# Transposing q, k and x with VectorE blocks and SBUF-to-SBUF DMAs instead of TensorE, in a fused attention and feed-forward kernel

## The chip, the cores and the metric

The kernel runs on one core of one Trainium2 chip. The metric is the device time of one execution in microseconds (us); lower is better. Before the change the median of three runs is 1325.62 us (1324.89 to 1325.84).

The names of the engines in the profile: PE is TensorE's matmul, PEld its weight load, DVE is VectorE, ACT is ScalarE, POOL is GpSimd, SP is SyncE, which here only issues DMAs. A q behind a name (SPq) is the engine's sequencer.

## The reference

128 short sequences of 32 positions with 512 channels go through one layer: a conditional mixing of channels, attention with a causal linear bias, an adapter matrix chosen by sequence, and a feed-forward part with a shared and a routed branch. All is float32.

```python
# _L0_cond_ref: each sequence has its own 32x32 matrix
W = weights[condition]
x1 = jnp.einsum('bct,bcd->bdt', x, W)

# _L0_attn_ref: 32 heads of 16
qkv = jnp.clip(jnp.einsum('bsd,ed->bse', x1, w_qkv), -8.0, 8.0)
q, k, v = jnp.split(qkv, 3, axis=-1)
q = _layer_norm(q, q_ln_w, q_ln_b)
k = _layer_norm(k, k_ln_w, k_ln_b)
scores = jnp.einsum('bqhd,bkhd->bhqk', q, k) * scale      # per head
scores = jnp.where(causal, scores + slopes * rel, -jnp.inf)
attn = jnp.einsum('bhqk,bkhd->bqhd', softmax(scores), v)
x = x + jnp.einsum('bsd,ed->bse', attn, w_out)

# _L0_cond2_ref: each sequence has its own 512x512 adapter
h = jnp.einsum('bsi,boi->bso', x, weight[adapter_ids])

# _L0_ffn_ref
top2 = jax.lax.top_k(jnp.einsum('bsh,he->bse', h, gate_w), 2)[0]
shared = jnp.einsum('bsi,ih->bsh', relu(h @ up_w) ** 2, down_w)
routed = ((h @ fc1_w) @ expert_w * sum(top2)) @ fc2_w
x = x + _layernorm(shared + routed, ln_gamma, ln_beta)
```

## The kernel before

The 4096 rows are cut into 32 tiles of 128 rows (128 partitions), so a tile holds four sequences of 32 positions (SEQ = 4, S = 32). Its 512 channels are four chunks of 128 (DC = 4). One loop runs over t = 0 to 33. In step t, tile t goes through its attention and its adapter, tile t+1 is mixed and projected ahead of it, and the feed-forward of tiles t-2 and t-3 is dealt out in eight pieces called fill(0) to fill(7): in even steps the eight column blocks of `up` for a pair of tiles (moving 256 columns at once), in odd steps the eight quarters of `down`, four for each tile of the pair.

What a tile passes through, with the lines that the profile names:

- `load` (L160, L162): x by a DMA on SP's queue, the condition's matrix by an indirect DMA on POOL's. `load_adapters` (L173, L190): the four sequences' ids into SP's registers, then eight DMAs of 512 KB on SP's queue into buffers that adapt of the tile before has to leave first.
- `mix` (L205, L213, L218): a block-diagonal mask by POOL, four matmuls (pxc), one copy to xcT by ACT.
- `project` (L230, L236, L242, L243): for i = 0, 1, 2 (q, k, v) four matmuls of 128x512, a clip by VectorE out of PSUM, and for q and k the statistics of the layer norm. `normalise` (L249): the layer norm without its weights, after a root by ACT and a reciprocal by VectorE (`rstd_of`, L153, L155).
- `turn` (L261, L263): eight 128x128 transposes of k and q by TensorE into two PSUM banks (pk, pq). `scale` (L273, L278, L282): the layer norm's weights, now per partition, by VectorE for k and by ACT for q, and kx, k copied out four times under a head mask.
- `scores` (L299, L306), `exponent` (L316, L317, L322), `share` (L327, L329, L330), `flip` (L338): q times k by heads, bias, maximum (VectorE), subtraction (POOL), exponential (ACT), sum and reciprocal (VectorE), product (POOL), and a transpose in 32x32 blocks by VectorE.
- `spread` (L349): v under a sequence mask by POOL. `weigh` (L362, L373): the probabilities times v (po), turned in blocks by VectorE (aT). `attend` (L382, L386): the output projection (pw), added to x by VectorE.
- `turn_x` (L392, L394, L395): four transposes of x by TensorE (px), a copy to xT by ACT, and POOL adds beta to x. `adapt` (L411, L416): for each of the four sequences in turn sixteen small matmuls with that sequence's adapter, and a VectorE transpose in 32x32 blocks into hT, which gathers the blocks in another order.
- `route` (L430, L437 to L443): the gate and the routed branch in two halves. `up` (L450, L455, L456) and `down` (L464). `finish` (L475 to L488): the sum, its layer norm and the store; `down` calls it after its last quarter. `routed_inner` and `routed_outer` multiply the routed branch's weights together once, at the start.

The instructions are written in an order by hand (the calls ahead of the loop and in it). The framework puts each on its engine's queue and sets the semaphores; where an operand comes late it may put a later, ready instruction first. Each queue then runs strictly in order. DMAs of SP's queue use eight semaphores in turn, so one waits until the DMA eight before it has landed. Dependencies go by the part of a tile that is read or written. PSUM has eight banks, which are handed out in turn.

Of the kernel before, what the change touches and what calls it, by code (L numbers as in the profile page):

```python
# [17 lines left out]
P = 128  # L18
# [12 lines left out]
NE = 8  # L31
# [10 lines left out]
def adaln_attn_ffn(  # L42
# [27 lines left out]
    def bank(name):  # L70
        return ps.tile([P, 512], F32, tag="ps", name=name)


    ident = const.tile([P, P], F32, name="ident")
    make_identity(nc, ident)
    eps = const.tile([P, 1], F32, name="eps")
# [168 lines left out]
    def normalise(t):  # L245
        s = tiles[t]
        r = rstd_of(s["mv"], 2, f"qk_{t}")
        for i in range(2):
# [4 lines left out]
            )  # L253

    def turn(t):

        s = tiles[t]
        s["pk"] = bank(f"pk_{t}")
        s["pq"] = bank(f"pq_{t}")
        for c in range(DC):  # L260
            nc.tensor.transpose(s["pk"][:, ts(c, P)], s["qk"][:, 1, ts(c, P)], ident)  # L261
        for c in range(DC):
            nc.tensor.transpose(s["pq"][:, ts(c, P)], s["qk"][:, 0, ts(c, P)], ident)  # L263

    def scale(t):

        s = tiles[t]
        s["qT"] = w1.tile([P, DC, P], F32, tag="qT", name=f"qT_{t}")
        kT = w1.tile([P, DC, P], F32, tag="kT", name=f"kT_{t}")

        s["kx"] = w1.tile([P, DC, SEQ, HQ, S], F32, tag="kx", name=f"kx_{t}")
        for c in range(DC):
            nc.vector.tensor_scalar(  # L273
                out=kT[:, c, :], in0=s["pk"][:, ts(c, P)],
                scalar1=lnc[:, 2, c : c + 1], scalar2=lnc[:, 3, c : c + 1],
                op0=ALU.mult, op1=ALU.add,
            )
            nc.scalar.activation(  # L278
                s["qT"][:, c, :], s["pq"][:, ts(c, P)], AF.Identity,
                bias=qaff[:, 1, c : c + 1], scale=qaff[:, 0, c : c + 1],  # L280
            )
            nc.vector.tensor_tensor(  # L282
                out=s["kx"][:, c],
                in0=kT[:, c, :].rearrange("p (b k) -> p b k", b=SEQ).unsqueeze(2)
                .broadcast_to([P, SEQ, HQ, S]),
                in1=m_half.unsqueeze(1).unsqueeze(3).broadcast_to([P, SEQ, HQ, S]),
                op=ALU.mult,
            )

    def scores(t):  # L290
# [4 lines left out]
        for c in range(DC):  # L295
            for b in range(SEQ):
                for r in range(2):
                    rows_r = slice(r * P // 2, (r + 1) * P // 2)
                    nc.tensor.matmul(  # L299
                        banks[r][ts(b, S), ts(c, HQ * S)],  # L300
                        lhsT=s["qT"][rows_r, c, ts(b, S)],
                        rhs=s["kx"][rows_r, c, b].rearrange("p h k -> p (h k)"),
                        start=True, stop=True,
                    )
# [53 lines left out]
    def weigh(t):  # L358
# [12 lines left out]

        s["aT"] = w1.tile([P, DC, SEQ, S], F32, tag="kT", name=f"aT_{t}")
        nc.vector.transpose(  # L373
# [14 lines left out]
    def turn_x(t):  # L388
        s = tiles[t]
        px = bank(f"px_{t}")  # L390
        for c in range(DC):
            nc.tensor.transpose(px[:, ts(c, P)], s["x"][:, ts(c, P)], ident)  # L392
        s["xT"] = w1.tile([P, DC, P], F32, tag="qT", name=f"xT_{t}")
        nc.scalar.copy(s["xT"].rearrange("p c n -> p (c n)"), px)  # L394
        nc.gpsimd.tensor_tensor(out=s["x"], in0=s["x"], in1=bet_sb, op=ALU.add)  # L395

    def adapt(t):
# [10 lines left out]
        for j in range(SEQ):  # L408
            for c in range(DC):
                for g in range(DC):  # L410
                    nc.tensor.matmul(  # L411
                        pad[ts(g, S), ts(j, P)], lhsT=s["xT"][:, c, ts(j, S)],
                        rhs=s["adw"][c // 2][j][:, c % 2, ts(g, P)],
                        start=(c == 0), stop=(c == DC - 1),
                    )
# [43 lines left out]
    def down(t, quarter):  # L459
# [3 lines left out]
        for f in range(2 * quarter, 2 * quarter + 2):  # L463
# [3 lines left out]
            )  # L467
        if quarter == 3:
            finish(t)

    def finish(t):

        s = tiles.pop(t)
        y = s["y"]
        nc.vector.tensor_tensor(out=y, in0=y, in1=s["pd"], op=ALU.add)  # L475
        st = sm.tile([P, 6], F32, tag="st", name=f"stf_{t}")
        nc.vector.bn_stats(out=st, in_=y)
        mv = sm.tile([P, 1, 2], F32, tag="mv1", name=f"mvf_{t}")
        nc.vector.bn_aggr(out=mv[:, 0, :], in_=st)
        r = rstd_of(mv, 1, f"f_{t}")  # L480
# [11 lines left out]
    load(0)  # L492
    for c in range(DC):
        for i in range(3):
            nc.sync.dma_start(
                out=wqkv_sb[:, c, ts(i, D)], in_=w_qkvT[c * P : (c + 1) * P, ts(i, D)]
            )
    load(1)
# [3 lines left out]
    for c in range(DC):  # L502
        for i in range(3):
            project(0, i, (c,))
    normalise(0)
    spread(0)
    nc.sync.dma_start(out=lnc, in_=ln_cols)
# [9 lines left out]
    load_adapters(0)  # L517
    nc.sync.dma_start(out=bet_sb, in_=beta.broadcast_to([P, D]))

    for g in range(DC):  # L520
        nc.sync.dma_start(
            out=rout_sb[ts(g, S), :, :NE], in_=gate_w[:, g, :].rearrange("(e d) n -> d e n", d=S)
        )
    for g in range(DC):
        nc.sync.dma_start(
            out=up_sb[ts(g, S), :, :],
            in_=up_w[g * P : (g + 1) * P, :].rearrange("(e d) f -> d e f", d=S),
        )
    nc.sync.dma_start(out=down_sb, in_=down_w.rearrange("(c p) f -> p c f", p=P))
    nc.sync.dma_start(out=gam_sb, in_=gamma.broadcast_to([P, D]))  # L530

# [4 lines left out]
    for t in range(NTILE + GRP):  # L536
        here, ahead, ffn = t < NTILE, t + 1 < NTILE, t >= GRP
        g = t // GRP - 1

        def fill(i):  # L540
            if t == 0 and i >= 4:
                routed_outer(i - 4)
            elif t == 1 and i == 3:
                mix(3)
            elif t == 1 and i >= 4:
                project(3, 0, (i - 4,))
            elif ffn and t % GRP == 0:
                up(g, i)
            elif ffn:
                down(g * GRP + i // 4, i % 4)  # L550

        if t + 2 < NTILE:
            load(t + 2)
        when(here and t > 0, load_adapters, t)
        when(here, turn, t)
        when(here, scale, t)
        when(ahead and t != 2, mix, t + 1)
        fill(0)
        fill(1)
        when(ffn, route, t - GRP, 0)  # L560
        when(here, scores, t)
        when(here, exponent, t)
        when(ffn, route, t - GRP, 1)
        when(ahead and t != 2, project, t + 1, 0)
        when(here, share, t)
        when(ahead, project, t + 1, 1)
        when(here, flip, t)
        fill(2)
        when(ahead, project, t + 1, 2)
        fill(3)  # L570
        when(here, weigh, t)
        when(ahead, normalise, t + 1)
        when(ahead, spread, t + 1)
        fill(4)
        when(here, attend, t)
        fill(5)
        when(here, turn_x, t)
        fill(6)
        fill(7)
        when(here, adapt, t)  # L580


# [75 lines left out]
```

## Time and profile before

| | us |
|---|---|
| median of the runs (3) | 1325.62 |
| the profiled execution | 1324.37 |
| its span, first to last instruction | 1322.4 |
| TensorE matmul busy (share 97%) | 1285.9 |
| VectorE busy (48%) | 640.6 |
| GpSimd busy (34%) | 447.0 |
| ScalarE busy (23%) | 303.0 |
| granted TensorE clock, mean | 0.991 |
| one step in the middle, e.g. from one px to the one two steps later, halved | 39.53 |

The costliest matmuls in the profile's groups are the projections (340.7 us busy), `up` (237.8) and `down` (237.7). Matmuls overlap in the array, so the mean duration of one (593 ns for a projection's) is longer than the distance from one to the next; distances between starts tell what a group costs. The loads from memory come to 153.93 MB, most of it adapters, 4 MB for each tile. The span can be read in three stages: up to about 101 us, where the first two tiles go through without feed-forward work; the steps 2 to 30; and from about 1243 us on, step 31 and the two last steps, which hold feed-forward work alone.

### The profile page before, as it was taken

To read this page: it belongs to the slowest core of one execution; us is meant where nothing else is said; L and a number is where in the kernel's file an instruction comes from. 1 tells how busy PE (TensorE), PEld (TensorE's weight loads), DVE (VectorE), ACT (ScalarE), POOL (GpSimd) and SP (SyncE) were. 2 spreads that over 40 slices of the span, in tenths; PEclk is the share of its full clock that TensorE was granted. 3 is DMA by queue.
4 is the path that set the end of the run, shared out by engine and by line. 5 is a ranking of instruction groups with operands and counts; after the bars stand their busy time and mean duration, and the time that the engine had idled before them with its cause. 6 is when DMAs were issued, how large, how long until landed. Compare 5 with 4: busy or idle time off the path is not lost.

```text
span 1322.4 us, 28001 instructions
## 1 busy us (share of the span) xinstructions
PE 1285.9 (97%) x11976; PEld 819.9 (62%) x11976; DVE 640.6 (48%) x1123; ACT 303.0 (23%) x552; POOL 447.0 (34%) x393
## 2 busy tenths in 40 slices
PE   5989999999999999999999999999999999999977
PEld 2447566665666756566665666756566665666655
DVE  2464553635545363653635545363653535455332
ACT  1222222121222222222121222212222121222211
POOL 4334333343323334323342324333333332323211
PEclk9989999999999999999999999999999999999989
DMA  9733343412434322343422334322343421334300
GB/s 317 201 121 127 128 161 129 141 68 97 145 129 161 129 71 90 130 159 129 159 73 76 143 129 160 129 97 75 133 146 128 161 88 74 127 128 144 128 17 16
DMA packets 51473, 164.12 MB, mean 124 GB/s; under 512 B 7061, under 2 KB 7830, under 8 KB 51350
## 3 DMA queue, kind: packets, MB, share of 16 engines
q1 hardware_dynamic: 47238, 153.15, 32.6%
q0 software_dynamic: 3424, 8.39, 1.6%
q8 instruction: 94, 1.54, 0.5%
q10 hardware_dynamic: 688, 0.79, 0.2%
q14 instruction: 29, 0.24, 0.0%
HBM read 153.93 MB, written 8.39 MB: 123 GB/s over the span
## 4 chain that ended last, share of the span: by engine, by line
PE 94%; DMA 4%; DVE 1%; issue 0%; POOL 0%; SPq 0%; ACTq 0%; POOLq 0%; DVEq 0%
PE pqkv L230 23%; PE pu L450 17%; PE pd L464 17%; PE pr L430 9%; PE pad L411 9%; PE pw L382 9%; PE psc L299 3%; PE po L362 2%; PE pxc L213 2%; PE pk L261 1%; DMA down_sb<-in_down_w 1%; PE px L392 1%; PE pq L263 1%; DMA bet_sb<-in_beta 1%; DMA fc_t<-in_fc_w 0%
## 5 line engine op out<-in xcount | busy, mean ns | idle before, releaser
L230 PE MATMUL pqkv<-wqkv_sb,xcT 128*128 128x512 f32 x768 | 340.7, 593 | 0.7 <-ACT xcT L218 0.7
L230 PEld LDWEIGHTS pqkv<-wqkv_sb,xcT 128*128 128x128 f32 x768 | 145.4, 190 | 163.7 <-issue 159.7
L450 PE MATMUL pu<-hT,up_sb 128*128 128x256 f32 x1024 | 237.8, 381 | 0.8 <-DVE hT L416 0.8
L464 PE MATMUL pd<-down_sb,act 128*128 128x512 f32 x512 | 237.7, 599 | 0.0
L450 PEld LDWEIGHTS pu<-hT,up_sb 128*128 128x128 f32 x1024 | 190.9, 190 | 45.8 <-issue 21.5
L349 POOL TENSOR_TENSOR vx<-v,msk 128x1024 f32<-128x1024 f32 x64 | 126.8, 2002 | 96.4 <-PE po L362 85.8
L464 PEld LDWEIGHTS pd<-down_sb,act 128*128 128x128 f32 x512 | 94.2, 191 | 101.6 <-issue 96.9
L456 POOL TENSOR_TENSOR act<-act 128x256 f32<-128x256 f32 x128 | 81.5, 636 | 188.9 <-ACT act L455 188.6
L430 PE MATMUL pr<-rout_sb,hT 128*128 128x256 f32 (+1 forms) x512 | 125.5, 389 | 0.0
L317 POOL TENSOR_TENSOR s<-s,mx 128x1024 f32<-128x1024 f32 x32 | 61.2, 1913 | 188.9 <-DVE mx L316 188.9
L382 PE MATMUL pw<-wout_sb,aT 128*128 128x512 f32 x256 | 117.6, 603 | 5.3 <-DVE aT L373 5.3
L411 PEld LDWEIGHTS pad<-adw,xT 128*32 128x32 f32 x4096 | 109.9, 110 | 17.7 <-issue 17.7
L455 ACT ACTIVATE act<-pu 128x256 f32<-128x256 f32 x128 | 49.2, 384 | 302.9 <-PE pu L450 302.9
L411 PE MATMUL pad<-adw,xT 128*32 128x128 f32 x4096 | 118.4, 273 | 0.0
L430 PEld LDWEIGHTS pr<-rout_sb,hT 128*128 128x128 f32 x512 | 94.8, 190 | 25.8 <-issue 13.6
L330 POOL TENSOR_TENSOR s<-s,rden 128x1024 f32<-128x1024 f32 x32 | 61.5, 1921 | 119.5 <-DVE rden L329 115.7
L236 DVE TENSOR_SCALAR qk<-pqkv 128x512 f32<-128x512 f32 x64 | 44.2, 691 | 106.1 <-PE pqkv L230 106.0
L416 DVE STREAM_TRANSPOSE hT<-pad 128x512 f32<-128x512 f32 x32 | 23.0, 717 | 145.4 <-PE pad L411 145.4
L382 PEld LDWEIGHTS pw<-wout_sb,aT 128*128 128x128 f32 x256 | 49.5, 194 | 62.6 <-issue 51.4
L282 DVE TENSOR_TENSOR kx<-kT,m_half 128x512 f32<-128x512 f32 x128 | 82.5, 684 | 0.0
L278 ACT ACTIVATE qT<-pq,qaff 128x128 f32<-128x128 f32 x128 | 48.2, 456 | 117.4 <-PE pq L263 117.4
L475 DVE TENSOR_TENSOR y<-y,pd 128x512 f32<-128x512 f32 x32 | 22.0, 688 | 99.0 <-PE pd L464 99.0
(63 smaller groups left out, 1145.1 us busy)
## 6 DMA issues: line engine op xcount, KB each, us to landing
adw<-in_adapt_w SPq DMA_DIRECT2D x256, 512.0 KB, 8.3
x<-in_x SPq DMA_DIRECT2D x32, 256.0 KB, 10.3
out<-y POOLq DMA_DIRECT2D x30, 256.0 KB, 3.6
wqkv_sb<-in_w_qkvT SPq DMA_DIRECT2D x12, 256.0 KB, 6.1
up_sb<-in_up_w SPq DMA_DIRECT2D x4, 512.0 KB, 7.7
down_sb<-in_down_w SPq DMA_DIRECT2D x1, 2048.0 KB
wout_sb<-in_w_outT SPq DMA_DIRECT2D x4, 256.0 KB, 7.9
fc_t<-in_fc_w ACTq DMA_DIRECT2D x1, 512.0 KB
```

The lines of the kernel that those rows point to most:

```text
L230: nc.tensor.matmul(s["pp", i], lhsT=s["xcT"][:, c, :], rhs=wqkv_sb[:, c, ts(i, D)], start=(c == 0), stop=(c == DC - 1),)
L282: nc.vector.tensor_tensor(out=s["kx"][:, c], in0=kT[:, c, :].rearrange("p (b k) -> p b k", b=SEQ).unsqueeze(2) .broadcast_to([P, SEQ, HQ, S]),
L317: nc.gpsimd.tensor_tensor(out=s["s"], in0=s["s"], in1=mx.unsqueeze(2).broadcast_to([P, H, S]), op=ALU.subtract,)
L330: nc.gpsimd.tensor_tensor(out=s["s"], in0=s["s"], in1=rden.unsqueeze(2).broadcast_to([P, H, S]), op=ALU.mult)
L349: nc.gpsimd.tensor_tensor(out=vx, in0=s["v"][:, ts(half, D // 2)].rearrange("p (h d) -> p h d", d=HD).unsqueeze(2) .broadcast_to([P, H // ...
L382: nc.tensor.matmul(pw, lhsT=s["aT"][:, g].rearrange("p b q -> p (b q)"), rhs=wout_sb[:, g, :], start=(g == 0), stop=(g == 3),)
L411: nc.tensor.matmul(pad[ts(g, S), ts(j, P)], lhsT=s["xT"][:, c, ts(j, S)], rhs=s["adw"][c // 2][j][:, c % 2, ts(g, P)], start=(c == 0), sto ...
L430: nc.tensor.matmul(pr[:, :n], lhsT=hT[:, c, ts(t % GRP, P)], rhs=rout_sb[:, c, ROUT[half] : ROUT[half + 1]], start=(c == 0), stop=(c == DC ...
L450: nc.tensor.matmul(pu[:, : GRP * P], lhsT=up_sb[:, c, ts(f, P)], rhs=pair["hT"][:, c, :], start=(c == 0), stop=(c == DC - 1),)
L455: nc.scalar.activation(a, pu[:, : GRP * P], AF.Relu)
L456: nc.gpsimd.tensor_tensor(out=a, in0=a, in1=a, op=ALU.mult)
L464: nc.tensor.matmul(s["pd"], lhsT=pairs[t // GRP]["acts"][f][:, ts(t % GRP, P)], rhs=down_sb[:, f, :], start=(f == 0), stop=(f == FC - 1),)
```

## The change

The transposes of `turn` and `turn_x` leave TensorE. A new helper `swap` does them in two moves: VectorE transposes every 32x32 block in place of its own (`blocks`), and 16 DMAs on SP's queue carry the blocks from one group of 32 partitions to another, j being the source group (the sequence) and i the target group. q and k go together, so one such DMA moves 32 partitions with two runs of 512 bytes; for x it is one run. The results stay in the order [sequence, chunk, position], and `scale`, `scores` and `adapt` read them so. `scale` works in place in SBUF. The identity matrix and the three PSUM banks go; aT gets a buffer of its own.

The order of the steps changes:

- `turn` and `scale` of tile t+1 are now in step t: `turn` after `normalise`, which follows `flip`, and `scale` after fill(4). A step begins with `scores`.
- `project(t+1, 2)` (v) and `spread` move behind `attend` and `turn_x`; `route`'s second half moves between `weigh` and `attend`; `project(t+1, 0)` and `(t+1, 1)` stay ahead of fill(2).
- `turn_x` comes ahead of v's projection and fill(4), where it came after fill(5).
- `finish` is cut in two: `total` (sum and statistics) at the old place, `finish` later, in the next step for the odd tile of a pair.
- Ahead of the loop the weights of q and k come before those of v, `turn(0)`, `mix(1)`, `project(1, 0)`, `project(1, 1)`, `scale(0)` and half of `routed_outer` are done; the loads of beta, gate, up, down and gamma are issued in step 0 after `turn(1)`. The work that fills steps 0 and 1 is dealt out anew.

```diff
+    def swap(srcs, name):
+        n = len(srcs)
+        blocks = w1.tile([P, n, DC, DC, S], F32, tag=f"blocks{n}", name=f"blocks_{name}")
+        out = w1.tile([P, n, SEQ, DC, S], F32, tag=f"T{n}", name=f"T_{name}")
+        for k, src in enumerate(srcs):
+            nc.vector.transpose(
+                out=blocks[:, k], in_=src.rearrange("p (c i d) -> p i c d", c=DC, i=DC)
+            )
+        for j in range(SEQ):
+            for i in range(DC):
+                nc.sync.dma_start(out=out[ts(i, S), :, j], in_=blocks[ts(j, S), :, i])
+        return out
+
     def turn(t):
         s = tiles[t]
-        s["pk"] = bank(f"pk_{t}")
-        s["pq"] = bank(f"pq_{t}")
-        for c in range(DC):
-            nc.tensor.transpose(s["pk"][:, ts(c, P)], s["qk"][:, 1, ts(c, P)], ident)
-        for c in range(DC):
-            nc.tensor.transpose(s["pq"][:, ts(c, P)], s["qk"][:, 0, ts(c, P)], ident)
+        s["T"] = swap([s["qk"][:, i, :] for i in range(2)], f"qk_{t}")
...
     def turn_x(t):
         s = tiles[t]
-        px = bank(f"px_{t}")
-        for c in range(DC):
-            nc.tensor.transpose(px[:, ts(c, P)], s["x"][:, ts(c, P)], ident)
-        s["xT"] = w1.tile([P, DC, P], F32, tag="qT", name=f"xT_{t}")
-        nc.scalar.copy(s["xT"].rearrange("p c n -> p (c n)"), px)
+        s["xT"] = swap([s["x"]], f"x_{t}")[:, 0]
         nc.gpsimd.tensor_tensor(out=s["x"], in0=s["x"], in1=bet_sb, op=ALU.add)
...
     normalise(0)
+    turn(0)
+    project(0, 2)
     spread(0)
...
     load_adapters(0)
+    mix(1)
+    project(1, 0)
+    project(1, 1)
+    scale(0)
+    for c in range(DC // 2):
+        routed_outer(c)
...
+        first = {
+            (0, 2): [(routed_outer, 2)], (0, 3): [(routed_outer, 3)],
+            (1, 2): [(project, 2, 2)], (1, 3): [(spread, 2)],
+            (1, 4): [(mix, 3)], (1, 5): [(project, 3, 0)],
+        }
+        done = {(1, 0), (1, 1), (2, 3), (3, 0)}
...
         if t + 2 < NTILE:
             load(t + 2)
         when(here and t > 0, load_adapters, t)
-        when(here, turn, t)
-        when(here, scale, t)
-        when(ahead and t != 2, mix, t + 1)
+        when(here, scores, t)
+        when(ahead and t not in (0, 2), mix, t + 1)
         fill(0)
+        when(here, exponent, t)
         fill(1)
+        when(t > GRP and t % GRP == 0, finish, t - GRP - 1)
         when(ffn, route, t - GRP, 0)
-        when(here, scores, t)
-        when(here, exponent, t)
-        when(ffn, route, t - GRP, 1)
-        when(ahead and t != 2, project, t + 1, 0)
+        look(0)
         when(here, share, t)
-        when(ahead, project, t + 1, 1)
+        look(1)
         when(here, flip, t)
+        when(ahead, normalise, t + 1)
+        when(ahead, turn, t + 1)
+        if t == 0:
+            late_loads()
         fill(2)
-        when(ahead, project, t + 1, 2)
         fill(3)
         when(here, weigh, t)
-        when(ahead, normalise, t + 1)
-        when(ahead, spread, t + 1)
+        when(ffn, route, t - GRP, 1)
+        when(here, attend, t)
+        when(here, turn_x, t)
+        when(ffn and t % GRP, finish, t - GRP - 1)
+        if t != 1:
+            look(2)
+            when(ahead, spread, t + 1)
         fill(4)
-        when(here, attend, t)
+        when(ahead, scale, t + 1)
         fill(5)
-        when(here, turn_x, t)
         fill(6)
         fill(7)
         when(here, adapt, t)
+    finish(NTILE - 1)
```

`look(i)` is `project(t + 1, i)`, left out where it is done already; `late_loads` holds the five weights' loads.

## The prediction

> **What bounds the kernel now.** I read the page from the top: busy time by slice, then the chain that ended last, then busy time by stage, then the groups of instructions, then a timeline of two steps.
>
> ```profile
> PE   5989999999999999999999999999999999999977
> DMA  9733343412434322343422334322343421334300
> PE 94%; DMA 4%; DVE 1%; issue 0%; POOL 0%; SPq 0%; ACTq 0%; POOLq 0%; DVEq 0%
> ```
>
> TensorE is busy everywhere but in the first and the last slices, and 94% of the chain lies on it. The busy time by stage makes that exact (columns: stretch, length, then busy time and instructions of PE, PEld, DVE, ACT and POOL, the granted clock, the DMA share, GB/s):
>
> ```profile
> 0.00:101.00 101.00, 78.71 (x737) 41.33 (x738) 43.67 (x69) 20.64 (x31) 37.03 (x39) 0.93 0.68 215
> 101.00:1243.00 1142.00, 1142.00 (x10792) 736.46 (x10793) 572.30 (x1007) 269.51 (x495) 398.60 (x341) 1.00 0.33 121
> 1243.00:1323.00 80.00, 65.16 (x451) 42.11 (x448) 24.62 (x48) 12.82 (x26) 11.40 (x13) 0.93 0.15 56
> ```
>
> From 101 to 1243 us TensorE isn't idle at all, at full clock. There, what is taken off TensorE comes off the time, one for one, unless a wait takes its place. VectorE is half free, the DMA engines two thirds.
>
> **What is removed.** The twelve 128x128 transposes of a tile. Their busy time, 21.4 + 19.7 + 19.3 us by their groups, counts overlaps of pipelined matmuls, so I take distances between starts instead:
>
> ```profile
> 681.76 0.60 PE L392 MATMUL px<-ident,x 128*128 128x128 f32 x4
> 682.20 3.62 PE L450 MATMUL pu<-hT,up_sb 128*128 128x256 f32 x16
> 685.75 3.70 PE L411 MATMUL pad<-adw,xT 128*32 128x128 f32 x128
> 689.38 0.65 PE L261 MATMUL pk<-ident,qk 128*128 128x128 f32 x4
> 690.31 1.06 PE L213 MATMUL pxc<-blk,x 128*128 128x128 f32 x8
> ```
>
> px costs 682.20 - 681.76 = 0.44 us, pk with pq 690.31 - 689.38 = 0.93 us: 1.37 us a tile, **43.8 us** over 32 tiles. (By the chain's shares, 1.3% + 1.1% + about 1%, it would be 45.) ACT's copy of xT (0.59) goes too, off the path.
>
> **What is added, VectorE.** Three transposes of 128x512 a tile; the nearest row is hT's, which also gathers blocks: 0.72 us, so 2.2 us in a step of 39.5 in which VectorE is busy for 20. Free in throughput; its latency is in the sums below. The scaling of k and q reads SBUF instead of PSUM; neither is on the path, as scores follow 5 us later (below).
>
> **What is added, DMAs.** 32 a tile on SP's queue, 32 KB each for q with k, 16 KB for x: 24 MB more in all, 0.75 MB a step. The DMA engines have room, and at the right place:
>
> ```profile
> 652.00:661.00 9.00, 9.00 (x99) 7.13 (x98) 5.19 (x10) 3.13 (x8) 3.36 (x5) 1.00 0.99 374
> 661.00:686.00 25.00, 25.00 (x156) 15.94 (x157) 8.82 (x15) 6.16 (x11) 11.58 (x10) 1.00 0.01 4
> ```
>
> A step's adapter matrices fill the engines for some 12 us, then nothing moves for 25. The moves of q and k fall into that gap, as they follow the second projection. What counts is how fast SP issues, since the queue keeps order: the 16 of x stand behind the 16 of q and k, and behind x the next adapters. Two lines' DMAs in the view by source line, and SP's timeline:
>
> ```profile
> L514 SPq DMA_DIRECT2D wout_sb<-in_w_outT x4: 311/312/332, 14.3 to 16.4; - x4
> L495 SPq DMA_DIRECT2D wqkv_sb<-in_w_qkvT x12: 328/434/738, 2.0 to 9.9; - x12
> 686.45 4.50 SPq L190 DMA_DIRECT2D adw<-in_adapt_w  x8
> ```
>
> (ns least, median, most.) A DMA into 32 partitions takes 0.31 us to issue (wout), one into 128 takes 0.43 (wqkv), 0.04 between two. So one costs between **0.36** and **0.47** us, or 0.56 if the 4.50 us of eight adapter loads with their register work were the measure. I take 0.36, wout's, the only ones that also fill 32 partitions. Landing: between 1.7 us (msk, 6 KB, idle engines) and 2.9 (x, 256 KB, the fastest); I take 2.0. A DMA also waits for the one eight before it, since eight semaphores go round (gam's 1.73 and x's 2.84 us of issue in the first 45 us are such jams); 8 x 0.36 = 2.9 us covers a landing of 2.0.
>
> The Trainium skill speaks against this: *DMA: Bandwidth & Descriptors*, section Rules for kernel authors, says to join many small transfers, as below 64 KB one pays mostly overhead. By its fixed 2.0 us for each DMA, paid one after another, 32 would be an estimated 64 us a step, far over the step. The trace has eight adapter loads issued in 4.50 us and in flight together, so I don't count it so.
>
> **Does it fit into a step?** Zero is the start of weigh's matmuls:
>
> ```profile
> 659.89 7.03 PE L230 MATMUL pqkv<-wqkv_sb,xcT 128*128 128x512 f32 x16
> 668.55 1.25 DVE L338 STREAM_TRANSPOSE pT<-s 128x1024 f32<-128x1024 f32 x1 [0.89 <-POOL s L330]
> 673.74 1.10 PE L362 MATMUL po<-vx,pT 128*32 128x64 f32 x64
> 680.24 0.69 DVE L386 TENSOR_TENSOR x<-x,pw 128x512 f32<-128x512 f32 x1 [4.61 <-PE pw L382]
> ```
>
> - q, k: in the new order the projection of k ends two fills (2 x 1.73) earlier, at -3.5. Before, from there to the end of normalise took 5.4 us (666.76 to 672.15, flip's 1.25 within). So 1.9; two transposes 3.4; aT's may come between: 4.1. SP issues from 4.1 to 9.9, landed 11.5. scale took 3.75 us (650.60 to 654.35): done by 15.3. scores(t+1) comes after adapt, at 20.2: 5 us spare.
> - x: attend's addition ends at 7.2, its transpose 7.9. SP is busy until 9.9, so x goes from 9.9, the last landing at 9.9 + 15 x 0.36 + 2.0 = 17.3. adapt starts at 6.3 (attend's end) + 3.43 (projection of v) + 4 x 1.72 = 16.6 and takes four sequences one after the other, 0.9 each; the last is wanted at 19.3. Spare: **2.0 us**.
> - SP then does x(t+3), the register loads (some 2 us) and the adapters, so these start some 2 us later than now; they're wanted a step later. What waits behind SP's waiting DMAs is only these.
> - probabilities: from the start of the two projections to flip's end it took 669.80 - 659.89 = 9.9 us. Now only two fills lie behind them: 6.87 + 3.45 = 10.3. Spare: **0.4 us**, before it was 3.9, because the projection of v moves behind attend. If it is late, weigh is, and all after it; cost between 0 and 0.5 us a step; in even steps finish's 1.7 us of VectorE come ahead of it. I take 0.1 us x 30 = **+3**.
> - hT: scores (1.1) and pxc (0.9) cover its 0.72 now, as pk, pq and pxc did. aT is covered by half a route, 1.73, as by a fill before. total takes finish's first three VectorE instructions, finish the rest; none of it is waited for by TensorE except through flip.
> - shapes: 0.34 us of gap stood ahead of scores, where it followed a route; now it follows adapt. Between -0.3 and +0.3 a step; I take 0.
>
> **The two ends.** At t = 31 weigh waited 6.72 us and the two groups after it ran slow (po 1.94 instead of 1.10, four pd 3.50 instead of 1.88). Now route's first half and four fills, 8.65 us, stand between scores and weigh, where 5.2 stood; the chain of softmax without the detour over tile 28's sums (which cost VectorE 0.9) needs 10.9. Wait left: 2.2, so -4.5; a wait of 1.58 at 48.15 didn't slow po (1.10), one of 4.22 at 88.17 did slow pw (5.99 instead of 3.60); 2.2 is nearer the first, so another -2.4. **-6.9**. At the start, the 5.61 us before pk and the 4.22 with its slow pw can be filled; against that, tile 0's softmax loses the projections that covered it (some 4 us), the first moves queue among 4 MB of adapters (up to 8), and 4.5 MB of late weights reach x's first moves. Between -10 and +10: I take **0**.
>
> **Sum.** The profiled execution took 1324.4 (span 1322.4, 2.0 around it): 1324.4 - 43.8 + 3 - 6.9 = 1276.7. The median of the runs shown lies 1.25 above the profiled one: **1278**. Own range, from the bounds of the start and the shapes: 1264 to 1292. Chance 0.63.
>
> **Rivals.**
> 1. SP's issue is the bound (slower). Place: x's moves, adapt waits. With d us a DMA the last lands at 4.1 + 31 d + 2.0; over 19.3 each 0.1 us of d costs 3.1 us a step. It starts at d = 0.43 and eats all of 1.37 at 0.47, the wqkv price: no gain but the ends', about 1319. At 0.52, between that and the adapters' 0.56, the wait is 2.9 us, 1.5 a step lost over 31: 1325.6 + 47 - 7 = **1366**. For it: 128-partition issues did cost that. Against: no 32-partition one did. Chance 0.16.
> 2. The softmax chain decides: weigh late by 0.5 to 1.5 us a step: 1278 + 30 x (0.4 to 1.4), **1290 to 1320**. For it: 0.4 us spare. Against: VectorE takes what is ready first, as seen at 668.55, where flip overtook bn_stats. Chance 0.17.
> 3. The waits just cancel the gain. Chance 0.04.
>
> I see nothing that would pull it below 1264. Faster by over 0.2% (2.7 us, what can be told from no change): 0.63 + 0.17 = 0.80; within: 0.04; slower: 0.16. The range for 8 in 10 takes in rival 2: 1264 to 1324.
>
> **What will tell.** No row for pk, pq, px; steps of about 38.2 us against 39.53. SP's new DMAs at 0.31 us each: right; at 0.45 or more, rival 1, with TensorE idle before pad on a DMA of T_x. Idle before po on pT: rival 2. Idle before psc on kx: the spare 5 us of scale were wrong. Idle in the first 100 us above the 22 of before: my zero was wrong.

## The result, and the profile after

The median went from 1325.73 us (four runs, 1324.89 to 1326.42) to **1534.19 us** (four runs, 1532.71 to 1535.05): a ratio of 1.157, interval 1.155 to 1.159. The profiled execution has a span of 1532.0 us, 209.6 more than before.

The page of the changed kernel, the rows that answer to those shown of before (TensorE and the DMA engines in 40 slices, the chain that ended last by engine and by line):

```profile
PE   7557889989898988889998998998988898888988
DMA  5753323343422434322443432334343133334210
PE 42%; SPq 39%; DMA 7%; DVE 6%; issue 4%; ACT 1%; POOL 0%; ACTq 0%; DVEq 0%; POOLq 0%
SPq L264 38%; PE pqkv L227 13%; PE pd L465 7%; PE pr L431 6%; DMA T_x<-blocks_x 5%; PE pu L451 5%; PE pad L412 4%; PE psc L304 3%; PE pxc L210 3%; DVE qk L246 2%; DVE blocks_qk L259 1%; DMA gam_sb<-in_gamma 1%; PE po L367 1%; DVE qk L233 1%; DVE st L239 1%
```

TensorE held 94% of the chain; now it has 42%, and 39% is SP's sequencer, nearly all of it at line 264, the `dma_start` inside `swap`. No slice of the middle has the DMA engines above 4 tenths, as before: issuing takes the time, not the bytes. Busy time by stage (stretch, length, then busy time and instructions of PE, PEld, DVE, ACT, POOL, granted clock, DMA share, GB/s):

```profile
0.00:110.00 110.00, 69.48 (x560) 34.19 (x560) 41.80 (x68) 16.61 (x26) 29.75 (x33) 0.84 0.65 203
110.00:1440.00 1330.00, 1183.87 (x10458) 745.97 (x10459) 646.38 (x1106) 251.65 (x467) 391.93 (x343) 0.94 0.36 121
1440.00:1532.00 92.00, 74.63 (x576) 49.09 (x574) 26.18 (x47) 12.24 (x26) 13.52 (x17) 0.88 0.18 63
```

In the middle TensorE is idle for 146 of 1330 us, and its granted clock is 0.94 where it was 1.00. By the starts of pad (adapt's matmuls) the loss falls into three parts, which add up to the 209.6:

| stretch | before | after | lost |
|---|---|---|---|
| start to pad of tile 2 | 132.6 | 172.2 | 39.6 |
| pad of tile 2 to pad of tile 31 (29 steps) | 1143.8 | 1304.9 | 161.1 |
| pad of tile 31 to the end | 46.0 | 54.9 | 8.9 |

In the stretch of 29 steps TensorE is idle for 138.1 us where it was 6.7, and busy for 1166.8 where it was 1137.1, although the transposes are gone. Both point at `pad`, whose group of matmuls, before and after, is this (count, then busy us and mean ns, then idle before and its releaser):

```profile
L411 PE MATMUL pad<-adw,xT 128*32 128x128 f32 x4096 | 118.4, 273 | 0.0
L412 PE MATMUL pad<-adw,T_x 128*32 128x128 f32 x4096 | 170.3, 318 | 143.7 <-DMA T_x<-blocks_x 143.4
```

Steps 4 to 30 (from the pad of tile 3 to that of tile 30) take 45.3 us on average (39.5 before; 38.2 forecast). Two of them, SP's timeline and then, of TensorE's, the projections of q and k and pad in the first of the two (start, length, engine, operation, count, idle before):

```profile
706.30 10.60 SPq L264 DMA_DIRECT2D T_qk<-blocks_qk  x16
717.00 10.08 SPq L264 DMA_DIRECT2D T_x<-blocks_x  x16
727.32 5.36 SPq L187 DMA_DIRECT2D adw<-in_adapt_w  x8
750.21 10.30 SPq L264 DMA_DIRECT2D T_qk<-blocks_qk  x16
760.61 10.56 SPq L264 DMA_DIRECT2D T_x<-blocks_x  x16
```

```profile
694.37 7.03 PE L227 MATMUL pqkv<-wqkv_sb,xcT 128*128 128x512 f32 x16
721.62 1.08 PE L412 MATMUL pad<-adw,T_x 128*32 128x128 f32 x32
723.37 1.08 PE L412 MATMUL pad<-adw,T_x 128*32 128x128 f32 x32 [0.67 <-DMA T_x<-blocks_x]
725.75 1.08 PE L412 MATMUL pad<-adw,T_x 128*32 128x128 f32 x32 [1.31 <-DMA T_x<-blocks_x]
728.44 1.08 PE L412 MATMUL pad<-adw,T_x 128*32 128x128 f32 x32 [1.61 <-DMA T_x<-blocks_x]
736.75 7.03 PE L227 MATMUL pqkv<-wqkv_sb,xcT 128*128 128x512 f32 x16
```

The loop closes through SP. From the projections of q and k (694.37) it is 11.93 us to the first move of q and k, 20.78 through both trains of sixteen, 1.36 from the last issue to the last quarter of pad, and 8.31 from there to the next projections: 42.4 for this step. Averaged over steps 4 to 30 the four parts are 12.68, 20.95, 1.75 and 9.95: 45.3. x's blocks were ready at 712.7 (attend's addition 711.28 to 711.97, its transpose 0.71) and stood 4.3 us behind the train of q and k. The other step takes 46.1: there `total`'s first addition (0.69, and it waits for `down`) came ahead of normalise on VectorE, and its bn_stats ahead of aT.

### The profile page after: what moved, and what is told of

Same layout as the page of the kernel before. It is cut to its first block, busy times and chain, and to the rows that moved or that the text cites. A ratio compares the mean times of both kernels' runs of the same rounds, so it can differ in the third digit from the quotient of the medians.

```text
span 1532.0 us, 28949 instructions
## 1 busy us (share of the span) xinstructions
PE 1328.0 (87%) x11592; PEld 829.2 (54%) x11592; DVE 714.4 (47%) x1219; ACT 280.5 (18%) x518; POOL 435.2 (28%) x391
## 4 chain that ended last, share of the span: by engine, by line
PE 42%; SPq 39%; DMA 7%; DVE 6%; issue 4%; ACT 1%; POOL 0%; ACTq 0%; DVEq 0%; POOLq 0%
SPq L264 38%; PE pqkv L227 13%; PE pd L465 7%; PE pr L431 6%; DMA T_x<-blocks_x 5%; PE pu L451 5%; PE pad L412 4%; PE psc L304 3%; PE pxc L210 3%; DVE qk L246 2%; DVE blocks_qk L259 1%; DMA gam_sb<-in_gamma 1%; PE po L367 1%; DVE qk L233 1%; DVE st L239 1%
## 5 line engine op out<-in xcount | busy, mean ns | idle before, releaser
L412 PE MATMUL pad<-adw,T_x 128*32 128x128 f32 x4096 | 170.3, 318 | 143.7 <-DMA T_x<-blocks_x 143.4
L412 PEld LDWEIGHTS pad<-adw,T_x 128*32 128x32 f32 x4096 | 130.7, 126 | 188.5 <-issue 150.7
L465 PE MATMUL pd<-down_sb,act 128*128 128x512 f32 x512 | 228.7, 595 | 1.0 <-issue 1.0
L451 PEld LDWEIGHTS pu<-hT,up_sb 128*128 128x128 f32 x1024 | 197.9, 195 | 42.0 <-issue 11.4
L284 ACT ACTIVATE T_qk<-T_qk,qaff 128x128 f32<-128x128 f32 x128 | 54.2, 483 | 314.5 <-DMA T_qk<-blocks_qk 282.8
L279 DVE TENSOR_SCALAR T_qk<-T_qk,lnc 128x128 f32<-128x128 f32 x128 | 69.7, 584 | 87.8 <-DMA T_qk<-blocks_qk 64.3
L492 POOL DMA_DIRECT2D out<-y x30 | 18.0, 600 | 297.2 <-DVE y L488 219.7
L288 DVE TENSOR_TENSOR kx<-T_qk,m_half 128x512 f32<-128x512 f32 x128 | 95.0, 781 | 0.0
L202 POOL TENSOR_TENSOR blk<-cw,msk 128x128 f32<-128x128 f32 x32 | 12.7, 396 | 279.6 <-PE pxc L210 278.6
L332 DVE TENSOR_REDUCE den<-s 128x32 f32<-128x1024 f32 x32 | 39.0, 1220 | 107.5 <-ACT s L327 107.5
L215 ACT COPY xcT<-pxc 128x512 f32<-128x512 f32 x32 | 18.7, 585 | 345.4 <-PE pxc L210 345.4
```

The costliest lines, as they stand in the source:

```text
L279: nc.vector.tensor_scalar(out=k[:, :, c], in0=k[:, :, c], scalar1=lnc[:, 2, c : c + 1], scalar2=lnc[:, 3, c : c + 1], op0=ALU.mult, op1=AL ...
L284: nc.scalar.activation(q[:, :, c], q[:, :, c], AF.Identity, bias=qaff[:, 1, c : c + 1], scale=qaff[:, 0, c : c + 1],)
L288: nc.vector.tensor_tensor(out=s["kx"][:, c], in0=k[:, :, c].unsqueeze(2).broadcast_to([P, SEQ, HQ, S]), in1=m_half.unsqueeze(1).unsqueeze( ...
L412: nc.tensor.matmul(pad[ts(g, S), ts(j, P)], lhsT=s["xT"][:, j, c], rhs=s["adw"][c // 2][j][:, c % 2, ts(g, P)], start=(c == 0), stop=(c == ...
L451: nc.tensor.matmul(pu[:, : GRP * P], lhsT=up_sb[:, c, ts(f, P)], rhs=pair["hT"][:, c, :], start=(c == 0), stop=(c == DC - 1),)
L465: nc.tensor.matmul(s["pd"], lhsT=pairs[t // GRP]["acts"][f][:, ts(t % GRP, P)], rhs=down_sb[:, f, :], start=(f == 0), stop=(f == FC - 1),)
```

## The experiments

The theory after the result: SP's issue is the bound; a move between two places of SBUF costs far more to issue than the loads from memory that the prediction took its price from. Rivals: the partition count or the shape of a move sets its price; landing or the engines do, not issue; the order of the steps does.

Where no interval is given there is one execution. The kernel before took 1327.3 us on the chip of the first two groups (micro to dram2), 1320.1 on those of the next two (start to dram4; dram5, dram6) and 1325.4 beside the last (sb5).

**micro: the price of one issue by itself.** It does nothing of the layer, only DMAs, each kind sixteen or eight times in a row from an otherwise idle kernel.

```diff
+    # SBUF to SBUF, 32 partitions, one run of 512 B
+    for m in range(16):
+        nc.sync.dma_start(out=t0[ts(m % 4, S), m], in_=a[ts(m // 4, S), m % 4])
+    # memory to SBUF, 32 partitions, one run of 512 B
+    for m in range(16):
+        nc.sync.dma_start(out=t1[ts(m % 4, S), m], in_=x[ts(m, S), 0:128])
```

> This kernel does none of the computation: it only issues groups of DMAs of 16 KB to 256 KB one after the other (SBUF to SBUF and memory to SBUF, into 32, 128 and 8 partitions, runs of 512 bytes, on SP's, ACT's and POOL's queues) and writes constants to the output. In the changed kernel SP spent 0.59 us on issuing each move between partition groups; before the change a load from memory into 32 partitions took 0.31. Theory A, the source decides (SBUF to SBUF): 0.59 us for every SBUF-to-SBUF group whatever its partitions, 0.33 for every load from memory, with the same 512-byte runs. Theory B, the shape decides (32 partitions, short runs): 0.59 for the loads from memory of this shape too, and another time for 128 partitions. Theory C, it is pressure from other traffic in the kernel: below 0.4 us here for all. ACT's queue: 0.59 under A.

By source line (durations in ns: least, median, most; then first and last start):

```profile
L78 SPq DMA_DIRECT2D sb_32x<-a x16: 507/597/656, 2.1 to 11.9; - x16
L82 SPq DMA_DIRECT2D hbm_32x<-in_x x16: 397/419/671, 0.7 to 18.3; - x16
L90 SPq DMA_DIRECT2D sb_128x2k<-a x8: 599/610/616, 29.0 to 33.6; - x8
L99 SPq DMA_DIRECT2D hbm_128x<-in_x x16: 334/430/432, 41.8 to 49.2; - x16
L103 ACTq DMA_DIRECT2D sb_32x_act<-a x16: 515/602/612, 2.0 to 11.7; - x16
L111 POOL DMA_DIRECT2D sb_32x_pool<-a x16: 496/496/631, 2.2 to 9.7; - x16
```

From memory 0.42 and 0.43 us, with 32 or 128 partitions alike; SBUF to SBUF 0.60, with 32 partitions of 512 bytes or 128 of 2 KB alike. The two ends decide, the shape doesn't. ACT's queue is no cheaper, POOL's is 0.50. In the changed kernel, with adapters and all, the same:

```profile
L264 SPq DMA_DIRECT2D T_qk<-blocks_qk x512: 585/595/1477, 28.9 to 1436.7; - x171
L264 SPq DMA_DIRECT2D T_x<-blocks_x x512: 507/589/1882, 71.7 to 1481.4; - x171
```

The median distance from one issue to the next is 0.64 us for q and k and 0.63 for x, so 32 moves hold SP for 20.3 us of every step (20.95 on average, as a few take longer).

**x_pe, qk_pe, order_pe: moves taken back.** In the changed order, x alone, q and k alone, or all three are transposed by TensorE again.

```diff
-        s["xT"] = swap([s["x"]], f"x_{t}")[:, 0]
+        px = bank(f"px_{t}")
+        for c in range(DC):
+            nc.tensor.transpose(px[:, ts(c, P)], s["x"][:, ts(c, P)], ident)
+        s["xT"] = w1.tile([P, SEQ, DC, S], F32, tag="xT", name=f"xT_{t}")
+        nc.scalar.copy(
+            s["xT"].rearrange("p j c d -> p c j d"), px.rearrange("p (c j d) -> p c j d", c=DC, j=SEQ)
+        )
```

> The changed kernel with x transposed by TensorE again (four transposes and ACT's copy); q and k keep VectorE and their 16 moves. Theory A (SP's two trains of 16 moves in a row set the step): with one train, q and k land at 4.1 + 16 x 0.635 + 1.9 = 16.2 after weigh's start, scaled by 20.7, where scores wants them at 20.2: step about 39, total 1290 to 1340, and no idle before pad on a DMA. Theory B (the new step order itself costs the time, the moves only wait in it): still above 1450.

> The changed kernel with q and k transposed by TensorE again (eight transposes); x keeps VectorE and its 16 moves. Theory A: x's train begins when x is ready, 7.9 us after weigh's start, and the last lands at 7.9 + 15 x 0.635 + 0.6 + 1.9 = 19.9 where 19.3 is wanted: a wait of under 1 us a step, total 1300 to 1350. Theory B (order): still above 1450.

> The changed kernel's step order with all twelve transposes of a tile by TensorE, none by VectorE, no moves. The two kernels with half of the transposes on TensorE showed that they stand where TensorE must wait for their operands in this order: pk 1.8 to 3.4 us for normalise, px 0.8 us for x, besides 1.1 us of pw for aT in odd steps. Theory A (the 32 moves' issue on SP costs the time): 39.5 + 1.8 to 3.4 + 0.8 + 0.5 = 42.6 to 44.2 a step, 1400 to 1460 in total, all of it idle ahead of pk, px and pw, and SP's chain share nil. Theory B (something else of the order): idle ahead of other matmuls.

Measured: x_pe 1379.84, qk_pe 1466.22, order_pe 1467.03, the first two above what was expected and the third just over it; qk_pe lies where its rival, the order of the steps, had put it (above 1450). What each takes away is gone: in x_pe pad has no wait at all, in qk_pe 31.7 us in total. But what each brings back stands in the wrong place. x_pe's px and the group rows of pk in qk_pe and order_pe (count, then busy us and mean ns, then idle before and its releaser):

```profile
714.66 3.60 PE L390 MATMUL pw<-wout_sb,aT 128*128 128x512 f32 x8
719.13 0.63 PE L400 MATMUL px<-ident,x 128*128 128x128 f32 x4 [0.87 <-DVE x L394]
```

```profile
L276 PE MATMUL pk<-ident,qk 128*128 128x128 f32 x128 | 24.3, 322 | 86.3 <-DVE qk L249 86.3
```

```profile
L276 PE MATMUL pk<-ident,qk 128*128 128x128 f32 x128 | 23.0, 309 | 88.9 <-DVE qk L249 88.9
```

In the new order a transpose follows its operand at once, so TensorE waits 0.87 us for x's addition and some 2.7 us a tile for normalise. The order makes room for moves and is bad for transposes; order_pe's steps take 44.0 us without a single move. So these three bracket nothing, and leave the order open as a cause; that it isn't the cause in the middle is shown by dram5 and sb5 below, which both have this order from step 3 on.

**x_act: x's moves on ACT's queue.**

```diff
-                nc.sync.dma_start(out=out[ts(i, S), :, j], in_=blocks[ts(j, S), :, i])
+                eng.dma_start(out=out[ts(i, S), :, j], in_=blocks[ts(j, S), :, i])
...
-        s["xT"] = swap([s["x"]], f"x_{t}")[:, 0]
+        s["xT"] = swap([s["x"]], f"x_{t}", nc.scalar)[:, 0]
```

> The changed kernel with x's 16 moves issued on ACT's queue, those of q and k on SP's. Theory A (serial issue on one queue is the bound): the two trains overlap, x's last move lands about 20 us after weigh's start, total 1290 to 1360, with ACT's relus and scalings later by up to 10 us. Theory C (the DMA engines or the landing are the bound, not the issuing): no gain, 1500 or more.

Measured 1551.71, no gain: a miss, and the value that the rival (engines or landing, not issue) had named. Of the loss against the changed kernel 13 us lie ahead of the pad of tile 2; steps 4 to 30 take 45.6 us. Timeline of SP, ACT's queue and TensorE in one step:

```profile
718.47 11.35 SPq L264 DMA_DIRECT2D T_qk<-blocks_qk  x16
734.39 9.89 SPq L187 DMA_DIRECT2D adw<-in_adapt_w  x8
```

```profile
724.91 11.44 ACTq L264 DMA_DIRECT2D T_x<-blocks_x  x16
736.40 0.38 ACT L456 ACTIVATE act<-pu 128x256 f32<-128x256 f32 x1 [15.91 <-PE pad L412]
```

```profile
741.96 1.93 PE L412 MATMUL pad<-adw,T_x 128*32 128x128 f32 x32 [5.46 <-DMA T_x<-blocks_x]
```

The trains overlap: x's starts when its blocks are ready, and its last move is issued 11.4 us later, where it was 14.4. But SP, free earlier, issues the next tile's adapters from 734.39 on, as pad's first quarters free their buffers, and the last quarter waits until 741.96, 5.6 us after the last issue, where it came 1.4 after it in the step shown of the changed kernel. That the adapters' 4 MB are ahead of it in the engines fits, but no run takes them away. So x_act alone doesn't decide between issue and landing; the next run and the two after it do. ACT meanwhile issues instead of working: the first relu of the last four pieces of `up`, which started at 726.68, comes at 736.40.

**x_more: eight more moves a tile**, x's own chunks into a spare tile that nobody reads, ahead of x's moves.

```diff
+        spare = w1.tile([P, 2, P], F32, tag="spare", name=f"spare_{t}")
+        for m in range(8):
+            nc.sync.dma_start(
+                out=spare[ts(m % DC, S), m // DC], in_=s["x"][ts((m + 1) % DC, S), ts(m % DC, P)]
+            )
         s["xT"] = swap([s["x"]], f"x_{t}")[:, 0]
```

> The changed kernel with eight more moves of 16 KB a tile on SP's queue, into a buffer that nothing reads, ahead of x's. Theory A (SP's issue sets the step): 8 x 0.635 = 5.1 us more a step, over 31 steps 157: about 1690. Theory C (the engines' or the landing's time sets it; 128 KB more at some 300 GB/s): 0.4 us a step, 1545. A bound elsewhere: 1534.

Measured 1631.07, +97 us over the changed kernel, 3.0 us a step where eight issues take 5.1: above either rival, below the theory. TensorE's timeline shows where the rest went:

```profile
766.15 1.94 PE L417 MATMUL pad<-adw,T_x 128*32 128x128 f32 x32 [4.52 <-DMA T_x<-blocks_x]
768.01 1.06 PE L304 MATMUL psc<-kx,T_qk 64*32 64x128 f32 x20
769.01 1.88 PE L417 MATMUL pad<-adw,T_x 128*32 128x128 f32 x32
770.82 0.66 PE L304 MATMUL psc<-kx,T_qk 64*32 64x128 f32 x30
772.25 1.08 PE L417 MATMUL pad<-adw,T_x 128*32 128x128 f32 x32 [0.76 <-DMA T_x<-blocks_x]
773.26 0.44 PE L304 MATMUL psc<-kx,T_qk 64*32 64x128 f32 x14
773.63 0.71 PE L210 MATMUL pxc<-blk,x 128*128 128x128 f32 x4
774.58 1.08 PE L417 MATMUL pad<-adw,T_x 128*32 128x128 f32 x32 [0.24 <-DMA T_x<-blocks_x]
```

The framework, which puts a ready instruction ahead of a late one, laid the next tile's scores between the quarters of pad, so less is left to do after the last quarter. Averaged over steps 4 to 30, against the changed kernel: both trains with the eight moves take 26.51 us (20.95), the way from the last quarter to the next projections 7.30 (9.95), and the other two parts of the loop 12.59 (12.68) and 1.93 (1.75). That is 5.56 more, 2.65 less and 0.09 from the rest: the 3.0. Issue is the bound; its slope is softened by what can be moved under it.

**dram and dram2: fewer and cheaper DMAs for the same transposition.** The blocks go into a buffer in memory by one write and come back by one read for each sequence (x) or sequence and operand (q, k): 14 DMAs a tile for 32. In dram2 x's write is issued by ACT, and `total` of a pair's first tile follows weigh.

```diff
+        far = dr.tile([P, n, DC, DC * S], F32, tag=f"far{n}", name=f"far_{name}")
+        eng.dma_start(
+            out=far.rearrange("p k i f -> p (k i f)"),
+            in_=blocks.rearrange("p k i c d -> p (k i c d)"),
+        )
         for j in range(SEQ):
-            for i in range(DC):
-                nc.sync.dma_start(out=out[ts(i, S), :, j], in_=blocks[ts(j, S), :, i])
+            for k in range(n):
+                nc.sync.dma_start(
+                    out=out[:, k, j].rearrange("p c d -> p (c d)"),
+                    in_=far[ts(j, S), k].rearrange("p i f -> i p f"),
+                )
```

> The changed kernel with its moves taken through a buffer in memory: one DMA writes all blocks there (512 KB for q and k, 256 KB for x), and reads by sequence bring them back, 8 for q and k, 4 for x, each into 128 partitions. 14 DMAs a tile instead of 32, none from SBUF to SBUF; by the DMA runs such a one costs SP 0.42 + 0.05 us, so 6.6 us a step instead of 20.3, with one more landing (about 3 us for the write) in each chain. Theory A: q and k back at 4.1 + 3.3 + 8 x 0.47 + 2 = 13.2 after weigh's start, x's last quarter at about 18, wanted 19.3: no wait ahead of pad; steps of about 38.5 (even) and 39.6 (odd, aT), 1280 to 1320 in total. If landing in memory takes over 5 us, pad waits again: over 1350.

> As the kernel before it, with x's write issued on ACT's queue, so that it doesn't stand behind the reads of q and k, and with the first tile's total put behind weigh, so that VectorE turns aT before it. Expected: no wait ahead of pad, none ahead of pw in odd steps; steps of 38.4, 1265 to 1300. A rival: ACT's write, and what waits behind it on ACT, comes late and pad waits: above the kernel without it.

Measured 1370.44 and 1338.21, both above what was expected but 164 and 196 below the changed kernel, although every byte now goes out to memory and back. SP's timeline in dram2:

```profile
735.53 0.34 SPq L264 DMA_DIRECT2D far_qk<-blocks_qk  x1
739.15 5.36 SPq L270 DMA_DIRECT2D T_qk<-far_qk  x8
746.09 2.16 SPq L270 DMA_DIRECT2D T_x<-far_x  x4
```

x's moves hold SP for 2.2 us where they held it for 10.1, and steps 4 to 30 take 39.25 us. What dram2 missed by is in part these steps (38.4 were expected) and in part the start: pad of tile 2 at 160.0, 27.5 later than in the kernel before.

**start, dram3, dram4: the start.** start and dram3 issue the first loads in another order, in the changed kernel and in dram2; dram4 is dram3 with x of the first two tiles and q, k of the first by TensorE.

```diff
+    nc.sync.dma_start(out=lnc, in_=ln_cols)
...
+    load_adapters(0)
     for l in range(LC):
         routed_inner(l)
     mix(0)
...
     turn(0)
+    late_loads()
     project(0, 2)
```

> The changed kernel with its start alone in another order: the loads of ln, fc1, bias, ids, wout and the first tile's adapters are issued ahead of mix(0), and those of beta, gate, up, down and gamma right after turn(0), so that SP no longer stands at turn(0)'s moves with the DMA engines idle. Changed kernel: pad(0) at 86.2 us, pad(2) at 172.2, whole 1534. Theory: the start is a term of its own; pad(0) comes 10 to 20 us earlier, pad(2) 5 to 20, the whole 1515 to 1530, and the steps in the middle stay at 45 us. Rival: the order of the steps (the chain of a tile with nothing to fill it), not the loads, sets the start: pad(0) moves by less than 5 us and the whole stays at 1530 to 1536.

> dram2 with the same order of loads at the start. dram2: pad(0) 83.5, pad(1) 124.6, pad(2) 160.0, whole 1338. Theory: pad(0) 70 to 75, pad(2) 143 to 152, steps in the middle as in dram2 (39.0), so 1318 to 1330, about the time of the kernel before. Rival (the chain of the first tiles sets the start): pad(2) at 155 or more, 1333 to 1340.

> dram3 with x of the first two tiles and q, k of the first tile still transposed by TensorE, which waits there anyway; from then on all through memory. Theory: 4 to 8 us off the chain of each of the two first tiles, pad(2) 130 to 142, the steps after it as in dram2, so 1305 to 1318, under the kernel before. Rival: transposes and copies find TensorE, VectorE and ScalarE no less late; 1318 to 1330 as dram3.

Measured: start 1527.57, pad of tile 2 at 161.5, 10.7 earlier, as its theory said; the whole is 6.6 lower, which says little, as the kernel before was 5.7 faster on this chip too. dram3's ratio is 1.0192 (1.0179 to 1.0205), pad of tile 2 at 165.3, 5 us later than in dram2, outside its theory and on the side of its rival; dram4's is 1.0071 (1.0049 to 1.0093), at 150.2, near its rival. The same edit helps one kernel and not the other: in dram3 the write of tile 0's q and k is issued behind the adapters at 29.4 and its first read at 36.4 (29.5 and 32.6 in dram2), and the first scores start at 47.7 instead of 42.3. TensorE's transposes in the first tiles bring 15 us. This fits a start that is in the main a chain of single tiles with little to fill it, which no run isolates; the order of the loads alone doesn't mend it.

**dram5 and dram6: the start of before, the middle of dram2.** Steps 0 to 2 and all ahead of the loop are as in the kernel before; from tile 3's q and k on the moves go through memory in the new order. dram6 has a seventh buffer for x.

```diff
+    OLD = 2
...
+        if t <= OLD:
+            turn(t)
+            scale(t)
...
+            normalise(t + 1)
+            when(t == OLD, turn, t + 1)
...
-    xp = ctx.enter_context(tc.tile_pool(name="xp", bufs=6))
+    xp = ctx.enter_context(tc.tile_pool(name="xp", bufs=7))
```

> Steps 0 to 2 and all ahead of the loop as in the kernel before (TensorE transposes, its order of loads and steps); from tile 3's q and k and step 3 on as in dram2 (moves through memory, the new order). Theory: the start is lost to the new order and its loads alone, so pad(2) comes at 132 to 134 as before, the steps from 3 on at 39.0 on average as in dram2 to dram4 (from pad(2) to the end 1181 there), so the ratio to the kernel before is 0.990 to 0.996. Rival: dram2's late steps come from work that the start put off, or step 3 pays for the change of order; ratio 0.998 to 1.006.

> dram5 with a seventh buffer for x. In dram4 a load of x stood between the write and the reads of q and k on SP's queue and waited 2.7 us for VectorE's last use of its buffer, and that step took 44.6 us. Theory: the buffer takes that wait away; no step over 41 us, the mean step 38.9 or less, ratio 0.002 to 0.004 below dram5's. Rival: another wait of the queue takes its place; same as dram5 within 0.001.

Measured: dram5 1306.09, ratio **0.989** (0.9875 to 0.9903); dram6 1303.08, 0.9885 (0.9867 to 0.9903). Both beat both kernels. pad of tile 2 comes at 128.7 and 128.8, steps 4 to 30 take 39.3 and 39.0 us. The seventh buffer is worth nothing that can be told: SP's waits ahead of x's load are still there (median 2.7 us), the late steps are gone only from the one profiled execution. The middle of dram6, by busy time and by TensorE's groups between 140 and 1260 us:

```profile
140.00:1260.00 1120.00, 1098.22 (x10316) 692.76 (x10316) 618.10 (x1085) 245.26 (x453) 382.04 (x330) 1.00 0.45 160
```

```profile
L485 PE MATMUL pu<-hT,up_sb 128*128 128x256 f32 x903 | 203.3, 381 | 7.2 <-DVE hT L451 7.2
L446 PE MATMUL pad<-adw,T_x 128*32 128x128 f32 x3712 | 107.7, 273 | 1.7 <-DMA T_x<-far_x 1.3 <-PE pu L485 0.3
L411 PE MATMUL pw<-wout_sb,aT 128*128 128x512 f32 x232 | 106.0, 600 | 7.7 <-DVE aT L402 7.7
```

The clock is back at 1.00, pad waits 1.7 us in all, and the 21.8 us that TensorE is idle are for the greater part waits for hT and aT.

**sb5: the path of the moves alone.** dram5 with `swap` as in the changed kernel.

> dram5 with the moves back to SBUF to SBUF, 32 of them a tile on SP's queue as in the changed kernel; all else as in dram5 (the kernel before's start, total behind weigh). Theory: the path of the moves is what costs in the middle: steps from 3 on at 44 to 46 us, pad(2) at 129, so 175 to 205 us above dram5, 1480 to 1510; SP's moves 0.63 us apart. Rival: a good part of the changed kernel's steps came from the start's order running on, or from total's place: steps of 43 or less, under 1450.

Measured 1499.97; pad of tile 2 at 133.7, steps 4 to 30 at 45.7 us, the distances between moves again 0.64 and 0.63. Against dram5 nothing in the program but the path differs: by the spans 191 us (1498.2 and 1306.9), 180 of them between the pads of tiles 2 and 31. The 5.0 ahead of them are a wait for aT with a slow pw in step 1, before any move goes out. The chips differ too, by 5.3 us for the kernel before. pad's group in sb5:

```profile
L438 PE MATMUL pad<-adw,T_x 128*32 128x128 f32 x4096 | 166.1, 314 | 118.8 <-DMA T_x<-blocks_x 118.7
```

## Why the prediction was wrong, point by point

**The step that failed** is the issue price, "one costs between 0.36 and 0.47 us, or 0.56": it measured 0.635 from one issue to the next. The rows it came from, wout and wqkv, are loads from memory; the move has both ends in SBUF, and the trace of before held no such DMA. The prediction sorted its rows by partitions (0.31 into 32, 0.43 into 128), which micro shows to be no cause: 0.42 and 0.43. The trace of before spoke against it too: the 256 adapter loads into 128 partitions have a median issue of 0.33, and wout's were not "the only ones that also fill 32 partitions" (those of the gate and `up` do, at 0.32 and 0.31). So the upper bound was no bound.

**The mechanism was rival 1's**, at its place (x's moves, adapt waits), at a price beyond its last row. Its own clock with 0.635: the last move lands at 4.1 + 31 x 0.635 + 2.0 = 25.8, 6.5 late; less the 1.37 saved, 5.1 a step, 148 us over the 29 steps between the pads of tiles 2 and 31. Measured: 161. That the two are so close is partly luck. TensorE waited for the moves only 115.4 us in these steps, 4.0 each: the first move went out 1.5 us (even steps) or 3.1 (odd) after weigh's start, not 4.1. What fills the sum up is in no term of the prediction: `pad`'s matmuls were busy 45.9 us longer, at a lower granted clock (last section), and pw waited 16.0 us on `total`'s sums. "None of it is waited for by TensorE except through flip" was wrong in odd steps, where `total` also puts the moves of q and k back.

**The start at "0" was the second wrong term**: +39.6 by the pad of tile 2, four times its bound of 10. "What will tell" named it: idle in the first 100 us above 22, and it is 39. dram5 with the old start has 128.7 instead of 172.2.

**Right:** VectorE's transposes cost 0.66 to 0.71 us, and little on the path (those of q and k have 1% of the chain). Landing, taken at 2.0, is 1.8 to 1.9. The eight semaphores don't jam (SP's distances stay at 0.635). Rival 2's chain is not what decides: po waits 10.1 us in all, mostly at the start. The tail's -6.9 is there once the moves are cheap: from the pad of tile 30 to the end dram5 takes 77.0 us and the kernel before 83.4, -6.4 (the changed kernel takes 90.5).

**Half right:** the 1.37 that leave TensorE. dram6 keeps 0.5 of them, with steps of 39.0, not 38.2. Of the other 0.9 a step some 0.8 is the 21.8 us of idle time shown above, so "scores (1.1) and pxc (0.9) cover its 0.72" for hT and half a route for aT were covers with small holes.

**The rule that spoke against the change** (the Trainium skill, *DMA: Bandwidth & Descriptors*, Rules for kernel authors: join small transfers) had the right sign, and dram2, with 14 for 32, bears it out. The estimate drawn from that page's fixed 2.0 us, which its section Anatomy of one DMA gives for DMAs that GpSimd issues, was 64 us a step, three times too much: the trains held SP for some 21 us a step, as landings overlap and issues on one queue don't. The same page says, under Issuing engines are not separate DMA queues, that the time on the sequencer to start a DMA is usually small beside the DMA. Here it was 0.60 us beside a landing of 1.8 to 1.9 and, in a train of 32, almost all.

## What to carry to other kernels

Price a DMA's issue from a row with the same two ends, and where the trace has none, let the upper end of the range lie well above every row, or measure sixteen in a row before building on them. On a queue in order it is the number of DMAs that counts, so sum (number x distance between issues) over all that stand ahead of the one that is waited for. And take an order that was made for one kind of work together with that work: here the old order with TensorE's transposes took 39.5 us a step, the new one 39.0 with cheap moves and 44.0 with those transposes.

## What the runs showed of the hardware that wasn't expected

- A DMA from SBUF to SBUF takes 0.60 us to issue on SP and on ACT and 0.50 on POOL, one from or to memory 0.42 or 0.43 by itself (0.33 to 0.51 in dram2). The size has no say: 8 partitions of 512 bytes took 0.62, 128 of 2 KB 0.61.
- A transposition out to memory and back was faster than one inside SBUF, by some 190 us in this kernel (sb5 against dram5); it needs 14 DMAs instead of 32, and each read costs 0.51 us to issue.
- Short waits cost clock as well. In the changed kernel pad's quarters take 1.08 us or, after some waits, 1.93, and its mean went from 273 to 318 ns a matmul, 52 us in all beside the 144 of idle time. Rows of one step, and the stretch in which the profile has the clock at half (the 0.50):

```profile
767.94 1.08 PE L412 MATMUL pad<-adw,T_x 128*32 128x128 f32 x32 [1.62 <-DMA T_x<-blocks_x]
769.87 1.93 PE L412 MATMUL pad<-adw,T_x 128*32 128x128 f32 x32 [0.84 <-DMA T_x<-blocks_x]
```

```profile
769.92:776.75 6.83, 5.77 (x129) 4.57 (x129) 0.72 (x1) 0.00 (x0) 0.60 (x1) 0.50 0.73 244
```

The Trainium skill (*TensorE: Matmul & The Clock Gate*, What's actually happening) puts half rate after an idle window of about 3.4 us. Here no single wait in the step before was longer than 1.62 (none between 180 and 1440 us longer than 3.1), and half rate came all the same, after waits of 1.62 and 0.84 with 1.08 of work between them. What rule the clock follows there these runs don't show.
